# Another order for the side work of a fused cross-attention and expert kernel

## Chip, cores and metric

The kernel runs on one core of a Trainium2 chip. The metric is the device time of one execution in microseconds (us), the median of several runs. The engines are called as the profile calls them: PE (TensorE matmuls; PEld are its weight loads), DVE (VectorE), ACT (ScalarE), POOL (GpSimd) and SP (SyncE, which here only issues transfers).

## What is computed

A tensor x (4 batches, 512 rows, 256 columns) and a context (4 batches, 1601 rows, 256 columns), all in float32, go through two rounds of cross-attention and a mixture of experts:

```python
x = x + L0_xattn(ctx, layernorm(x))   # 8 heads of 128, queries from x, keys and values from ctx and x
x = x + L0_ffn(layernorm(x))          # 8 experts, top 2, capacity, tanh-GELU, 256 -> 1024 -> 256
x = x + L1_xattn(ctx, layernorm(x))   # 8 heads of 32, keys and values from ctx alone
x = x + L1_ffn(layernorm(x))          # 8 experts, top 2 with ties, GELU with biases
```

The second attention, which the change is mostly about, is `softmax(q k^T) v` for 512 queries and 1601 keys in 8 heads, for each of the 4 batches. The second mixture of experts routes each row to its two best experts and adds their weighted results.

## The kernel before, in words

The kernel has four parts that run one after the other, with some work pulled ahead: the first attention (to about 1585 us), the first feed-forward (to 1911 us), the second attention (to about 2537 us), and the second feed-forward (to the end).

**First feed-forward.** `all_experts` runs the 8 experts twice, once for each half of the slots. Per expert it calls `hidden` (32 matmuls and four GELUs on ACT), `turned` for the next expert, and `results` for the one before. After each of these three it takes one step of a generator with side work, so that a half has 24 steps, and one more is taken behind the last `results`. In the second half the generator is `keys_next`: keys and values of batch 1 (15 steps, a yield after every third), the queries of batch 0 (`queries`, 10 yields), and the first ten `maxima` calls. Each call fills two PSUM tiles of the pool `ps_s` with scores and has DVE reduce them to row maxima, which the softmax of the second attention subtracts.

**Second attention.** There are 16 units: batch b, key half o, query half f. Each has 13 steps, one for each block of 128 keys, so that a batch takes 52 steps (`per_batch`) and all four take 208. The loop goes two steps at a time; such a pair is called an iteration here. An iteration issues, in this order: `weights` for its two steps (scores into `ps_w`, then the exponential on ACT), `weigh` for the two steps before (their product with the values, into `ps_o`), `maxima` for a later unit (mostly one call, sometimes two), `add_weights` (two DVE adds that build the softmax sum; steps 0 and 12 of a unit have none), and last whatever is put down in the table `at` for the two steps. The four computing engines keep exactly this written order (`in_order`): an instruction that waits holds all that stands behind it on its engine. Transfers on SP are ordered by the planner.

The side work that `at` holds:

- `closing` of a unit: PE sums, a copy on ACT, PE transposes, three DVE operations into x.
- `keys_values(b + 1)` (generator `projected`): the context of a batch is loaded into `cw`, then 15 steps of matmuls, each into one PSUM tile that ACT copies out.
- `collect(b + 1)` gathers the results of the first experts by indirect DMA on POOL; `add_collected` adds them to x on DVE, one row tile at a time.
- `queries(b + 1)`: a layer norm with its square root on ACT (`ln_root`), PE transposes, two projections. Batch b + 1's are made during batch b.
- `route2(b - 1)`: the routing of the finished batch: layer norm, transposes, logits, top two, places, and 16 indirect scatters on POOL into `rows_a` and `rows_b`.
- `clear_rows`: on steps 4 to 44, transfers that clear these rows, each second one behind a memset on POOL.

The first PSUM tile that side work takes in an iteration comes from a pool of its own (`ps_m`, one buffer); further ones come out of the ring of three of `ps_s`, which `weights` and `maxima` use too (class `Beside`).

**Second feed-forward.** The rows of its first two experts are fetched from `rows_a` at step 202 (`load_first_rows`), turned at step 206 (`turn_first`), and put through the first layer at steps 210 and 213 (`first_layer`). Then 21 tiles of rows follow: for each, `hidden`, preparations of the next, and `results` of the one before, whose two products are scaled on DVE and added to the output by an indirect DMA on POOL (`add_out`). `route2` of the last batch and a planning table run beside. In this part, and in the first feed-forward, a planner chooses the order of instructions on each engine from when it thinks that inputs will be ready; `tc.keep_in_program_order(ins)` holds one instruction behind everything written before it for its engine.

Of the kernel before, what the change touches and what calls it, by code (L numbers as in the profile page):

```python
# [10 lines left out]
AF = mybir.ActivationFunctionType  # L11
# [6 lines left out]
B, S, D = 4, 512, 256  # L18
M = 1601
NT = S // P  # L20
# [20 lines left out]
FC = FF // P  # L41
# [33 lines left out]
def xattn_ffn_twice(ctx: ExitStack, tc: tile.TileContext, a: dict, out: bass.AP):  # L75
    nc = tc.nc
# [60 lines left out]
        nc.vector.tensor_scalar(ve, mv[:, :, 1], EPS, None, ALU.add)  # L137
        return ve

    def ln_root(pool, mv, n, ve=None):  # L140
        if ve is None:
            ve = ln_variance(pool, mv, n)
        rs = pool.tile([P, n], F32, tag=f"rs{n}", name="rs")
        nc.scalar.activation(rs, ve, AF.Sqrt)
        return ve, rs

    def ln_scale(pool, mv, n, root=None):
# [258 lines left out]
    def route2(b, two, psum, tag, first=0, n=NT):  # L406
# [7 lines left out]
        ve = ln_variance(two, mv, n)  # L414
        yield

        root = ln_root(two, mv, n, ve)
        yield
        mv, rs = ln_scale(two, mv, n, root)
        yield  # L420
# [707 lines left out]
    def queries(b, qT):  # L1128
        xn = soon.tile([P, NT, D], F32, tag="xn", name="xn")
        mv = ln_moments(turns, x[b], NT, some=())  # L1130
        for i in range(NT):
            ln_moments(turns, x[b], NT, mv=mv, some=(i,))
            if i + 1 < NT:
                yield
        ve = ln_variance(turns, mv, NT)
        yield

        root = ln_root(turns, mv, NT, ve)
        yield
        mv, rs = ln_scale(turns, mv, NT, root)  # L1140
        for i in range(NT):
            ln_apply(xn, x[b], mv, rs, i)
            if i in (0, NT - 1):
                yield
        xnT = soon.tile([P, DC, S], F32, tag="xnT", name="xnT")
        transposed(banks["beside"], "s", xnT, xn, NT)
        yield
        for o in range(DC):
            ps = banks["beside"].tile([P, 512], F32, tag="s", name="ps_q1")
            for c in range(DC):  # L1150
                nc.tensor.matmul(
                    ps,
                    lhsT=wT[:, 0, c, o * P : (o + 1) * P],
                    rhs=xnT[:, c, :],
                    start=c == 0,
                    stop=c == DC - 1,
                )
            nc.scalar.activation(qT[:, o, :], ps, AF.Copy, scale=DH1**-0.5)
            yield

    kvs = []
# [3 lines left out]
    def load_queries(u):  # L1165
        b, o, f = units[u]
        for pair in range(2):
            for s in range(2):
                i = 2 * pair + s
                nc.sync.dma_start(  # L1170
                    asked[u % 3][64 * s : 64 * s + 32, pair, :],
                    qTs[b][i * DH1 : (i + 1) * DH1, o, f * QH : (f + 1) * QH],
                )
# [60 lines left out]
    def begin(b):  # L1234
        qTs[b] = turns.tile([P, DC, S], F32, tag="qT", name="qT")
# [6 lines left out]
    with ExitStack() as st:  # L1242
# [30 lines left out]
        def hidden(e, half, sxT, w1, w2):  # L1273
            hT = two.tile([P, FC, HALF], F32, tag="hT", name="hT")
            for f0 in range(0, FC, 2):
                ps = ps_h.tile([P, 2, HALF], F32, tag="h", name="ps_h")
                for f in range(2):
                    for c in range(DC):
                        nc.tensor.matmul(  # L1279
                            ps[:, f, :],  # L1280
                            lhsT=w1[:, c, (f0 + f) * P : (f0 + f + 1) * P],
                            rhs=sxT[:, c, :],
                            start=c == 0,
                            stop=c == DC - 1,
                        )
                nc.scalar.activation(hT[:, f0 : f0 + 2, :], ps, AF.Gelu_apprx_tanh)  # L1286
            return e, half, hT, w2
# [86 lines left out]
        def keys_next():  # L1374
            *kv, steps = keys_values(ps_s, "s", 1)
            kvs.append(kv)
            for k, f in enumerate(steps):
                if k == 6:
                    add_collected(0, got0)
                f()  # L1380
                if k % 3 == 2:
                    yield
            begin(0)
            for _ in queries(0, qTs[0]):
                yield
            load_queries(0)
            for g in range(len(pieces)):
                maxima(0, g)
                yield
            negated(0)  # L1390
            for g in range(3):
                maxima(1, g)
                yield
                if g == 0:
                    to_row(0)
# [11 lines left out]
    def hidden_some(w, xT, hT, f0, ps):  # L1407

        n = xT.shape[-1]
        for f in range(2):  # L1410
            for c in range(DC):
                at = c * FF + (f0 + f) * P
                nc.tensor.matmul(
                    ps[:, f, :n],
                    lhsT=w(at, P),
                    rhs=xT[:, c, :],
                    start=c == 0,
                    stop=c == DC - 1,
                )
        for f in range(2):  # L1420
            nc.scalar.activation(
                hT[:, f0 + f, :], ps[:, f, :n], AF.Gelu, bias=w(WB2 + f0 + f, 1)
            )
# [6 lines left out]
    with ExitStack() as st:  # L1430
# [161 lines left out]
        def put(step, *fs):  # L1592
            at.setdefault(step, []).extend(fs)

        def spread(step, gen, every=1, count=8):
            for k in range(count):
                put(step + k * every, lambda: next(gen, None))
# [3 lines left out]
        def place(step, gen, offsets):  # L1601
            for k in offsets:
                put(step + k, lambda: next(gen, None))
            ends.append(gen)

        for u in range(1, n_units):

            put(NM * u - 7, lambda u=u: negated(u))
            put(NM * u - 5, lambda u=u: to_row(u))
            put(NM * u - 12, lambda u=u: load_queries(u))  # L1610
        for b in range(B):
            s0 = per_batch * b
            if b:
                put(s0 - 10, lambda b=b: load_keys(b, 0))
                put(s0, lambda b=b: load_keys(b, 1))

                beside = (4, 8, 10, 18, 20, 22, 24, 28, 30, 32, 34, 36, 38, 40, 42, 44, 46)
                bare = (4, 8, 10, 12, 12, 14, 14, 16, 18, 20, 22, 24, 26, 28, 30, 32, 34)
                steps = beside if b + 1 < B else bare
                place(s0, route2(b - 1, one, side, "s"), (*steps, *range(steps[-1] + 2, 54, 2), *range(54, 62)))  # L1620
            if b + 1 < B:
                put(s0 + 1, lambda b=b: begin(b + 1))
                got, steps = collect(b + 1)

                for k, f in enumerate(steps):
                    put(max(s0 - 28, 0) + 1 + k, f)
                for t in range(NT):
                    put(
                        s0 + 10 + 2 * t,
                        lambda b=b, got=got, t=t: add_collected(b + 1, got, (t,)),  # L1630
                    )

                def later(b=b):
                    yield from queries(b + 1, qTs[b + 1])

                place(s0, later(), range(12, 32, 2))
            if 1 <= b and b + 1 < B:

                def projected(b=b):
                    *kv, steps = keys_values(side, "s", b + 1, nc.scalar.copy)  # L1640
                    kvs.append(kv)
                    yield
                    for f in steps:
                        f()
                        yield

                spread(s0 + 2, projected(), 2, 16)
        put(per_batch * (B - 1) + 4, load_first_weights)
        put(NM * n_units - 6, load_first_rows)
        put(NM * n_units - 2, turn_first)  # L1650
# [58 lines left out]
    with ExitStack() as st:  # L1709
# [61 lines left out]
            turned_rows(rows, xT, tp)  # L1771
            return xT

        def hidden(w, xT, two=two):

            n = xT.shape[-1]
            hT = two.tile([P, FC, G], F32, tag="hT2", name="hT2")[:, :, :n]
            for f0 in range(0, FC, 2):
                hidden_some(w, xT, hT, f0, ps_h.tile([P, 2, G], F32, tag="h", name="ps_h2"))
            return hT  # L1780

# [190 lines left out]
        next(rest)  # L1972
        for i in range(n):
            w, xT, to, share = here
            hT = hidden(w, xT) if i else first_h
            for _ in range(3):
                next(rest, None)
            if more:
                fetched.append(more.pop(0)())
            if i + 1 < n:  # L1980
                here = ready(*fetched.pop(0))
            next(rest, None)
            if last:
                results(*last)
            next(rest, None)
            last = (w, to, share, hT, T - S if i < E else T)
            if i == n - 3:

                counts_i = one.tile([P, 4], I32, name="counts_i")
                tc.keep_in_program_order(nc.vector.tensor_copy(counts_i, state["counts"]))  # L1990
# [129 lines left out]
```

## Time and profile before

| what | value |
|---|---|
| median of 3 runs | 2819.07 us (2818.01 to 2824.54) |
| the profiled execution | 2825.64 us, of which the span of the trace is 2823.9 us |
| mean granted PE clock | 0.983 |
| PE busy | 2711.7 us, 96% of the span |
| DVE busy | 1458.4 us, 52% |
| ACT busy | 939.3 us, 33% |
| POOL busy | 262.4 us, 9% |
| exponentials of the second attention (208), on ACT | first at 1914.4 us, last at 2521.4 us |
| ACT table loads before the root in `ln_root` (line 144) | 20, of 1283 ns each |

PE's share is an average over parts with different limits, so it does not say where time can be won; the second attention has to be read by batch and by iteration. A trace row gives the start, the duration, engine, line, operation and tiles, and in brackets how long the engine had been idle before and what ended that. The page's own chain of waits covers only the last transfers of this program (each of its shares is 0%), so that stretches and single waits of the trace are read instead.

### The profile page before, as it was taken

To read this page: it belongs to the slowest core of one execution; us is meant where nothing else is said; L and a number is where in the kernel's file an instruction comes from. 1 tells how busy PE (TensorE), PEld (TensorE's weight loads), DVE (VectorE), ACT (ScalarE), POOL (GpSimd) and SP (SyncE) were. 2 spreads that over 40 slices of the span, in tenths; PEclk is the share of its full clock that TensorE was granted. 3 is DMA by queue.
4 is the path that set the end of the run, shared out by engine and by line. 5 is a ranking of instruction groups with operands and counts; after the bars stand their busy time and mean duration, and the time that the engine had idled before them with its cause. 6 is when DMAs were issued, how large, how long until landed. Compare 5 with 4: busy or idle time off the path is not lost. (4 is left out here: it accounts for less than half of the span.)

```text
span 2823.9 us, 35983 instructions
## 1 busy us (share of the span) xinstructions
PE 2711.7 (96%) x13566; PEld 1853.8 (66%) x13566; DVE 1458.4 (52%) x2307; ACT 939.3 (33%) x1362; POOL 262.4 (9%) x292
## 2 busy tenths in 40 slices
PE   6999999999999999999999999998999998889998
PEld 3667676666666676666676687874454454458887
DVE  6444556544476445455444412137887878872111
ACT  4323234232333233332332211114444444442221
POOL 0000000100001000001000001001110202022542
PEclk9999999999999999999999999999999999999999
DMA  5444343433343433334434555525621111025573
GB/s 172 116 112 116 97 113 86 111 95 92 93 120 89 106 96 95 96 82 107 98 91 125 166 174 172 173 80 156 176 68 40 38 30 56 31 77 188 163 219 103
DMA packets 196435, 311.95 MB, mean 110 GB/s; under 512 B 43319, under 2 KB 117368, under 8 KB 193560
## 3 DMA queue, kind: packets, MB, share of 16 engines
q1 hardware_dynamic: 157512, 227.52, 29.4%
q0 software_dynamic: 14160, 46.31, 5.6%
q10 hardware_dynamic: 24576, 35.68, 4.9%
q8 instruction: 111, 1.82, 0.3%
q14 instruction: 76, 0.62, 0.1%
HBM read 111.73 MB, written 51.34 MB: 58 GB/s over the span
## 5 line engine op out<-in xcount | busy, mean ns | idle before, releaser
L852 DVE TENSOR_REDUCE top<-ps_s 128x1 f32<-128x2113 f32 x128 | 301.8, 2358 | 587.3 <-PE ps_s L844 587.3
L881 PE MATMUL ps_o<-pT,v 128*128 128x256 f32 x2176 | 521.6, 381 | 0.5 <-DVE inv L859 0.5
L844 PE MATMUL ps_s<-kT,qT 128*128 128x512 f32 (+1 forms) x1280 | 489.0, 526 | 5.8 <-ACT attn L858 5.8
L881 PEld LDWEIGHTS ps_o<-pT,v 128*128 128x128 f32 x2176 | 409.9, 191 | 115.2 <-issue 68.4
L858 ACT ACTIVATE attn<-ps_s,top 128x2113 f32<-128x2113 f32 x128 | 259.0, 2024 | 478.8 <-DVE top L852 435.3
L844 PEld LDWEIGHTS ps_s<-kT,qT 128*128 128x128 f32 x1280 | 241.6, 190 | 252.4 <-issue 237.2
L873 DVE STREAM_TRANSPOSE pT<-swapped 128x2176 f32<-128x2176 f32 x128 | 312.4, 2440 | 33.4 <-DMA swapped<-attn 22.7
L1205 DVE TENSOR_REDUCE tops<-ps_s 128x2 f32<-128x1024 f32 (+1 forms) x224 | 238.3, 1105 | 107.4 <-PE ps_s L1194 106.3
L793 PE MATMUL ps_k<-kvin,wkv 128*128 128x512 f32 (+1 forms) x640 | 262.7, 533 | 3.8 <-DVE mv_g L731 2.1
L1463 PE MATMUL ps_w<-asked,keyed 64*128 64x256 f32 (+1 forms) x1664 | 227.8, 408 | 35.0 <-DVE tops L1205 35.0
L827 PE MATMUL ps_v<-wkv,kvin 128*128 128x256 f32 x1088 | 254.6, 381 | 1.3 <-ACT v L834 1.3
L1476 ACT ACTIVATE pT<-ps_w 128x1024 f32<-128x1024 f32 x192 | 189.8, 1022 | 154.1 <-PE ps_w L1463 138.5
L827 PEld LDWEIGHTS ps_v<-wkv,kvin 128*128 128x128 f32 x1088 | 204.7, 190 | 36.8 <-ACT v L834 6.3
L1463 PEld LDWEIGHTS ps_w<-asked,keyed 64*128 64x128 f32 (+1 forms) x1664 | 151.6, 189 | 113.4 <-DVE tops L1205 55.6
L1481 DVE TENSOR_TENSOR sum<-sum,pT 128x1024 f32<-128x1024 f32 x176 | 214.7, 1220 | 13.5 <-PE ps_o L1490 4.9
L806 ACT ACTIVATE kT<-ps_k,bqk 128x512 f32<-128x512 f32 (+1 forms) x160 | 96.8, 620 | 262.9 <-PE ps_k L793 122.4
L793 PEld LDWEIGHTS ps_k<-kvin,wkv 128*128 128x128 f32 x640 | 115.8, 191 | 77.6 <-issue 67.0
L834 ACT COPY v<-ps_v 128x512 f32<-128x512 f32 x144 | 79.7, 560 | 216.6 <-PE ps_v L827 148.3
L1194 PE MATMUL ps_s<-kv,qT 32*128 32x512 f32 (+1 forms) x1024 | 137.0, 561 | 8.8 <-DVE tops L1205 5.1
L1279 PE MATMUL ps_h<-sxT,w 128*128 128x256 f32 x512 | 116.1, 384 | 4.0 <-ACT hT L1286 4.0
L1293 PE MATMUL ps_y<-w,hT 128*128 128x256 f32 x512 | 116.8, 384 | 0.0
L1279 PEld LDWEIGHTS ps_h<-sxT,w 128*128 128x128 f32 x512 | 97.9, 192 | 20.8 <-ACT hT L1286 4.8
(306 smaller groups left out, 2516.1 us busy)
## 6 DMA issues: line engine op xcount, KB each, us to landing
swapped<-attn SPq DMA_DIRECT2D x1536, 68.0 KB
swapped<-attn ACTq DMA_DIRECT2D x512, 68.0 KB
w<-in_w_dram SPq DMA_DIRECT2D x32, 1024.0 KB
rows_b<-empty SPq DMA_DIRECT2D x36, 530.0 KB
w_e<-in_wall_dram SPq DMA_DIRECT2D x5, 2052.0 KB
cw<-in_ctxT_dram SPq DMA_DIRECT2D x4, 1601.0 KB
keyed<-kv SPq DMA_DIRECT2D x32, 200.1 KB
ctx_b<-in_ctx_dram SPq DMA_DIRECT2D x3, 1536.0 KB
```

What stands on the lines that cost most here:

```text
L793: nc.tensor.matmul(ps[:, :n], lhsT=wkv[:, c, hs], rhs=kvin[:, c, : NB - 1, k, :] if k < 4 else kvin[:, c, NB - 1, :, :], start=c == 0, sto ...
L827: nc.tensor.matmul(ps[:, k, :], lhsT=flat_kvin[c][:, j * P : (j + 1) * P], rhs=wkv[:, c, cols], start=c == 0, stop=c == DC - 1,)
L844: nc.tensor.matmul(flat[:, j0 : j0 + n], lhsT=qT[:, t * P : (t + 1) * P], rhs=kT[:, j0 : j0 + n], start=True, stop=True,)
L852: nc.vector.tensor_reduce(top, flat[:, :L], AX.X, ALU.max, negate=True)
L858: nc.scalar.activation(attn[:, :L], flat[:, :L], AF.Exp, bias=top, accum_out=total)
L873: nc.vector.transpose(pT[:, :, k * P : (k + 1) * P].rearrange("p c (a i) -> p a c i", a=4), swapped.rearrange("p a (c i) -> p a c i", i=32),)
L881: nc.tensor.matmul(ps, lhsT=v[:, j - parts[part][0], (h % 2) * DH0 : (h % 2 + 1) * DH0], rhs=pT[:, j, :], start=j == 0, stop=j == NB - 1,)
L1205: nc.vector.tensor_reduce(tops[u][:, t : t + at // n, 2 * pair : 2 * pair + 2, j0 // 512], of, AX.X, ALU.max,)
L1279: nc.tensor.matmul(ps[:, f, :], lhsT=w1[:, c, (f0 + f) * P : (f0 + f + 1) * P], rhs=sxT[:, c, :], start=c == 0, stop=c == DC - 1,)
L1463: nc.tensor.matmul(ps[:r, s, pair * QH : (pair + 1) * QH], lhsT=keyed[o][64 * s : 64 * s + 64, pair, j * P : j * P + r], rhs=asked[u % 3][ ...
L1476: nc.scalar.activation(pT[:r], ps[:r], AF.Exp)
L1481: nc.vector.tensor_tensor(sums[u, 0], sums[u, 0], pT, ALU.add)
```

## The change

Five things change.

1. **Second attention, keys and values.** The 15 steps of `keys_values` move from every second step (4 to 32 of a batch) to every third (6 to 48). Their generator is now `project`.
2. **Second attention, queries.** In batch 0, queries of batch 1 stay where they were (steps 10 to 34). Those of batch b + 1 for b of 1 and 2 begin 12 steps before batch b instead of 12 steps into it, with the adds of collected rows ahead of them; the gathers move by one step. `begin`, which takes the query tile, moves along (generator `ask`).
3. **Second attention, routing.** `route2` begins at step 0 of a batch instead of 4 and goes on in even steps; for the last batch it ends 6 steps earlier in the written order, at 45 instead of 52.
4. **First feed-forward.** `keys_next` yields after every fourth key step instead of every third, and the square root in the layer norm of batch 0's queries is kept behind what is written before it on ACT (`behind`).
5. **Second feed-forward.** The square root in the last batch's routing is kept in the same way. For the last tile of rows, `results` of the one before is called in the middle of `hidden`, after four of eight column groups, instead of behind it.

```diff
-    def ln_root(pool, mv, n, ve=None):
+    def ln_root(pool, mv, n, ve=None, behind=False):
...
-        nc.scalar.activation(rs, ve, AF.Sqrt)
+        root = nc.scalar.activation(rs, ve, AF.Sqrt)
+        if behind:
+            tc.keep_in_program_order(root)
...
-        root = ln_root(two, mv, n, ve)
+        root = ln_root(two, mv, n, ve, behind=b == B - 1)
...
-        root = ln_root(turns, mv, NT, ve)
+        root = ln_root(turns, mv, NT, ve, behind=b == 0)
...
-                if k % 3 == 2:
+                if k % 4 == 3:
                     yield
...
+        def ask(b):
+            begin(b)
+            yield
+            yield from queries(b, qTs[b])
+        def project(b):
+            *kv, steps = keys_values(side, "s", b, nc.scalar.copy)
+            kvs.append(kv)
+            yield
+            for f in steps:
+                f()
+                yield
...
-                beside = (4, 8, 10, 18, 20, 22, 24, 28, 30, 32, 34, 36, 38, 40, 42, 44, 46)
-                bare = (4, 8, 10, 12, 12, 14, 14, 16, 18, 20, 22, 24, 26, 28, 30, 32, 34)
-                steps = beside if b + 1 < B else bare
-                place(s0, route2(b - 1, one, side, "s"), (*steps, *range(steps[-1] + 2, 54, 2), *range(54, 62)))
+                even = (0, 6, 8, 12, 14, 18, 20, 24, 26, 28, 30, 32, 34, 36, 38, 40, 42, *range(44, 62))
+                bare = (0, *range(6, 37, 2), *range(37, 54))
+                place(s0, route2(b - 1, one, side, "s"), even if b + 1 < B else bare)
             if b + 1 < B:
-                put(s0 + 1, lambda b=b: begin(b + 1))
                 got, steps = collect(b + 1)
+                first = s0 + 10 if b == 0 else s0 - 12
                 for k, f in enumerate(steps):
-                    put(max(s0 - 28, 0) + 1 + k, f)
+                    put(first - (9 if b == 0 else 14) + k, f)
                 for t in range(NT):
                     put(
-                        s0 + 10 + 2 * t,
+                        first + 2 * t,
                         lambda b=b, got=got, t=t: add_collected(b + 1, got, (t,)),
                     )
-                def later(b=b):
-                    yield from queries(b + 1, qTs[b + 1])
-                place(s0, later(), range(12, 32, 2))
+                place(first, ask(b + 1), (0, *range(2, 26, 2)))
             if 1 <= b and b + 1 < B:
-                spread(s0 + 2, projected(), 2, 16)
+                place(s0, project(b + 1), (2, *range(6, 51, 3)))
...
-        def hidden(w, xT, two=two):
+        def hidden(w, xT, two=two, between=lambda: None):
...
             for f0 in range(0, FC, 2):
+                if f0 == FC // 2:
+                    between()
...
-            hT = hidden(w, xT) if i else first_h
+            if i == 0:
+                hT = first_h
+            elif i < n - 1:
+                hT = hidden(w, xT)
+            else:
+                hT = hidden(w, xT, between=lambda: results(*last))
+                last = None
```

More of the change, by code (lines that the diff above doesn't have):

```diff
@@ L1615, in xattn_ffn_twice @@
                 put(s0, lambda b=b: load_keys(b, 1))
-                beside = (4, 8, 10, 18, 20, 22, 24, 28, 30, 32, 34, 36, 38, 40, 42, 44, 46)
-                bare = (4, 8, 10, 12, 12, 14, 14, 16, 18, 20, 22, 24, 26, 28, 30, 32, 34)
-                steps = beside if b + 1 < B else bare
-                place(s0, route2(b - 1, one, side, "s"), (*steps, *range(steps[-1] + 2, 54, 2), *range(54, 62)))
+                even = (0, 6, 8, 12, 14, 18, 20, 24, 26, 28, 30, 32, 34, 36, 38, 40, 42, *range(44, 62))
+                bare = (0, *range(6, 37, 2), *range(37, 54))
+                place(s0, route2(b - 1, one, side, "s"), even if b + 1 < B else bare)
             if b + 1 < B:
-                put(s0 + 1, lambda b=b: begin(b + 1))
                 got, steps = collect(b + 1)
+                first = s0 + 10 if b == 0 else s0 - 12
                 for k, f in enumerate(steps):
-                    put(max(s0 - 28, 0) + 1 + k, f)
+                    put(first - (9 if b == 0 else 14) + k, f)
                 for t in range(NT):
                     put(
-                        s0 + 10 + 2 * t,
+                        first + 2 * t,
                         lambda b=b, got=got, t=t: add_collected(b + 1, got, (t,)),
                     )
-                def later(b=b):
-                    yield from queries(b + 1, qTs[b + 1])
-                place(s0, later(), range(12, 32, 2))
+                place(first, ask(b + 1), (0, *range(2, 26, 2)))
             if 1 <= b and b + 1 < B:
[L1639 to L1645, printed above, removed]
-                spread(s0 + 2, projected(), 2, 16)
+                place(s0, project(b + 1), (2, *range(6, 51, 3)))
         put(per_batch * (B - 1) + 4, load_first_weights)
```

## The prediction

> **What bounds it now.** I read the page's busy times first (PE 96% of the span), then the second attention (1911 to 2522 us) batch by batch in the view of busy times by stretch, cut where the first exponential of a batch starts. Columns: length, then busy us of PE, weight loads, DVE, ACT, POOL, the granted clock, DMA.
>
> ```profile
> 1914.40:2053.70 139.30, 126.34 (x1152) 63.96 (x1150) 117.50 (x137) 66.61 (x81) 21.62 (x46) 0.96 0.68 175
> 2053.70:2219.90 166.20, 153.38 (x1322) 85.43 (x1324) 139.25 (x225) 76.87 (x103) 21.12 (x27) 1.00 0.18 48
> 2219.90:2389.10 169.20, 158.05 (x1324) 86.57 (x1324) 136.78 (x223) 76.90 (x103) 17.95 (x16) 0.96 0.11 29
> ```
>
> The middle batches (rows two and three) are 27 and 30 us longer than batch 0, and neither PE nor DVE fills them: they take turns in being late. The same view for one plain iteration (two steps) and a loaded one of batch 1:
>
> ```profile
> 2049.00:2053.70 4.70, 4.22 (x40) 1.90 (x40) 4.59 (x5) 2.04 (x2) 0.10 (x1) 1.00 0.66 186
> ...
> 2142.10:2152.20 10.10, 9.81 (x76) 4.96 (x76) 4.09 (x4) 4.13 (x7) 0.00 (x0) 1.00 0.04 12
> ```
>
> Plain: DVE full, PE stalls. Loaded: PE full, DVE idle for 6 us. An iteration costs its busier engine.
>
> **The spread, worked out.** Prices are distances between starts in the timeline. PE: two ps_w 1.84, two weighings 1.0, one maxima 1.07, so 3.9 plain; a key or value step 1.75; query transposes 1.9, each projection 1.75; routing's transposes 1.9 and logits 1.8; closing 1.03, then 0.65. DVE: two reduces 2.28 and two adds 2.46, so 4.74 plain; a collected tile 1.03; a row tile's moments 0.64; closing 1.15. For each of the 104 iterations I added up what its two steps hold, took the larger sum, and summed. Against the measured lengths (last iteration left out):
>
> | batch | measured | rule before | rule after |
> |---|---|---|---|
> | 0 | 139.3 | 135.1 | 140.8 |
> | 1 | 166.2 | 163.2 | 160.3 |
> | 2 | 169.2 | 163.2 | 155.1 |
> | 3 | 131.4 | 121.7 | 121.4 |
> | sum | 606.1 | 583.2 | 577.6 |
>
> Batch 1, by steps from its start: steps 26 to 31, where query transposes and projections, routing's transposes and logits, key steps and a closing meet, fall from 27.8 to 19.3 (-8.5), and 10 to 19, which lose the next queries' tiles, by 5.3. Steps 6 to 9 rise by 3.2 (projections beside routing and the first keys), 40 to 45 by 5.1 (the queries two ahead, beside the last routing). The rest gives +2.6 net. Batch 2 takes on no queries at its end: hence -8.1; batch 0 takes them on: +5.7. **Taken: -5.6.** The rule leaves 23 us of waits in before; I let them stay. Ends: a better-spread order removes up to a third of each middle batch's excess over 145 us (DVE's own sum there), -14 for two; or new waits take +10.
>
> Moved DMAs. The context load (cw, 1601 KB) waits for the last key step: that moves from step 32 to 48, and the next first use is at 58, five iterations (about 28 us) on; on SP the loads of keys and queries behind it are for steps 65 and later: 0. The gathers of slot_y move one step, the adds that use them from 62 to 40; on POOL they stand between memsets that wait 7 us each, and before's last gather was issued at 2016.7, with the step-40 iteration at 2025: one memset more (2021.8) still precedes step 46 (2040): 0. Without that cover each late gather would hold DVE, some 5 us.
>
> **Routing's scatters (new wait).** Before, the first rows are fetched after six of batch 2's eight rows_a scatters; bare now ends at 45, so step 202 stands behind all eight.
>
> ```profile
> SPq L1580 <- DMA rows_a<-pay,place_a: 6.3, 1, 6.3
> ...
> 2522.23 0.66 PE L1404 MATMUL tp_f<-ident,cw 128*128 128x128 f32 x4
> ```
>
> The first line is SP's wait before the fetch. By POOL's timeline the sixth scatter went at 2507.46, the fetch at 2510.2, and its last reader was done before 2516.3. The first place comes one iteration later (4.3 us: first scatter 2497 instead of 2492.7); at 3.0 per pair the eighth goes at about 2518, lands near 2521, and the fetch is in at 2523.5 to 2526.6, where PE turns the rows at 2522.2. Behind that transpose on PE stand the last weighing and the first expert. **Taken +2** (0 to +4.4).
>
> **The pinned root of batch 0's queries.** ACT, then PE, in the timeline of the first feed-forward:
>
> ```profile
> 1755.02 1.28 ACT L144 ACT_TABLE_LOAD   x1
> 1760.62 0.20 ACT L144 ACTIVATE rs<-ve 128x4 f32<-128x4 f32 x1 [4.32 <-DVE ve L137]
> ...
> 1762.79 3.78 PE L1279 MATMUL ps_h<-sxT,w 128*128 128x256 f32 x8 [3.72 <-ACT hT L1286]
> ```
>
> The root was queued ahead of GELUs whose matmuls were done, and waited there for moments behind gathers. Pinned behind expert 2's work (some 40 us on) it finds its input ready, and ACT is idle 8.5 us between experts' GELUs. **Taken -3.7**, the whole gap; 0 if PE meets the next wait at once, -5 at most.
>
> **Keys in fours.** Two yields fewer put the last maxima inside the last expert instead of behind it:
>
> ```profile
> 1911.11 3.64 PE L1463 MATMUL ps_w<-asked,keyed 64*128 64x256 f32 x16 [2.54 <-DVE tops L1205]
> ```
>
> The 2.54 goes. Next late is the last result's copy (0.69), beside the first weights. But two full maxima now stand side by side, for which PE lost 0.73 idle and 1.1 in stretched matmuls (2.26 against 1.14) at 1850, where before's last such pair is a small and a full one. **Taken -1.2** (-2.5 to 0).
>
> **The last root.** ACT, then PE, where the last feed-forward begins:
>
> ```profile
> 2533.74 1.28 ACT L144 ACT_TABLE_LOAD   x1 [1.21 <-DVE earlier L500]
> 2535.04 0.20 ACT L144 ACTIVATE rs<-ve 128x4 f32<-128x4 f32 x1
> 2535.26 1.28 ACT L1421 ACT_TABLE_LOAD   x1
> 2536.55 0.84 ACT L1421 ACTIVATE cw<-ps_f,w_kv 128x256 f32<-128x256 f32 x2
> ...
> 2537.45 1.11 PE L1404 MATMUL tp<-ident,cw 128*128 128x128 f32 x4 [4.06 <-ACT cw L1421]
> ```
>
> By the rows the detour is 1.28 + 0.20 + 1.28 = 2.8 us: each function starts 1.3 after its load's start. [...] The rows decide: PE gets at most 3.2 (the GELU could start at 2533.4). But expert 1's matmuls (2539.41) also wait for DVE's copy of xT, which stood behind the norm that the root feeds; with that order kept only 0.3 is won. The planner sees a later root and may turn them round. **Taken -2** (-3.2 to -0.3).
>
> **The last results early.** POOL in the timeline of the end:
>
> ```profile
> 2804.50 1.56 POOL L1798 DMA_INDIRECT out_dram<-y,to  x1 [4.24 <-DVE y L1812]
> 2809.04 1.56 POOL L1798 DMA_INDIRECT out_dram<-y,to  x1 [2.98 <-DMA out_dram<-y,to]
> 2813.45 1.56 POOL L1798 DMA_INDIRECT out_dram<-y,to  x1 [2.85 <-DMA out_dram<-y,to]
> ```
>
> Each adding DMA follows the one before by 4.4 to 4.5. Half of hidden (1.86) moves behind results, so the third-last y is ready at 2802 and its DMA goes at 2803.2; then 2807.7 and 2812.2. **-1.2** (0 to -1.5).
>
> **Sum.** -5.6 + 2 - 3.7 - 1.2 - 2 - 1.2 = -11.7. The profiled execution took 2825.64 (span 2823.9 and 1.74 around it), 6.6 above the median of the runs, 2819.07. The same difference gives 2813.9 for it and **2807** for the median.
>
> **Rivals.** (1) *The spread gives nothing*: two sums of some 580 differ by 5.6 where 23 stay unexplained. For it: DVE's total is the same. Then -6, 2813: no change. (2) *It gives more*: PE may run one ps_w ahead of DVE (0.9 us), so lone key steps vanish in DVE's time, and the waits of crowded iterations go with the crowd. A third to a half of the middle batches' excess (21 and 24 us): 2795. Against: projections still meet keys and routing. (3) *Slower: DVE's side work ahead of its reduces.* A later iteration's reduces queue behind it, and PE needs the ps_s buffers that they free:
>
> ```profile
> 2409.46 1.94 PE L1194 MATMUL ps_s<-kv,qT 32*128 32x512 f32 x4 [2.39 <-DVE tops L1205]
> ```
>
> There 2.4 us of moments and closing stood in front. After, some 19 iterations hold queries' tiles beside routing or closing, or two or more side tiles. Five paying 2.4 each cancel the gain, nine make it slower by over 0.3%; ten give 2831. Against: before's steps 10 to 16 of batch 0 hold the same tiles and kept within 3 us of the rule together. (4) *The pins are moot*, the planner leaving both gaps: 2813, within (1).
>
> **Numbers.** A change under 0.3% (8.5 us) is within what runs of this kernel tell apart. Forecast (2801 to 2810.6) 0.36, (2) 0.24, (1) with (4) 0.25, (3) 0.15: faster 0.60, same 0.25, slower 0.15. The range, 2794 to 2824, leaves out a tenth at each side.
>
> **What would show it.** Batches 0 to 2 at about 145, 163 and 161 us; no 10-us iterations at a middle batch's steps 28 to 31; no PE gap at 1759, 1909 or of 4 us near 2533; a gap ahead of tp_f; the last POOL DMAs 4.5 apart. Wrong: batch 1 above 170, or DVE waiting on g.

## The result, and the profile after

The changed kernel takes **2811.86 us**, median of 11 runs (2800.23 to 2820.83), against 2819.64 us for the kernel before in the same comparison (2816.81 to 2826.92): ratio 0.9963, interval 0.995 to 0.9976. It is faster by 0.37%. The two profiled executions stand at 2825.64 and 2816.91 us (spans 2823.9 and 2815.2), both at a mean granted clock of 0.983. Against the -11.7 forecast, the medians differ by -7.8 us and the two spans by -8.7.

Busy times by stretch of the changed kernel, cut as before at the first exponential of each batch (columns as before: length; busy us of PE, weight loads, DVE, ACT, POOL; granted clock; DMA):

```profile
1913.40:2058.30 144.90, 127.26 (x1149) 64.98 (x1151) 123.54 (x155) 69.65 (x84) 22.38 (x51) 0.95 0.65 171
2058.30:2228.70 170.40, 160.22 (x1324) 87.30 (x1322) 137.72 (x224) 76.93 (x105) 27.82 (x33) 0.95 0.19 53
2228.70:2391.90 163.20, 156.47 (x1320) 85.48 (x1316) 130.95 (x206) 74.00 (x101) 16.83 (x16) 0.97 0.10 26
2391.90:2516.40 124.50, 113.14 (x1101) 64.77 (x1103) 109.41 (x179) 61.11 (x76) 17.24 (x15) 0.96 0.13 43
```

Batch 1 (second row) is the surprise: 170.4 us, four more than before, where 163 was forecast. "Batch 1 above 170" was one of the two signs named beforehand of being wrong; the other, DVE waiting on g, did not occur. The column to read beside it is the clock: 0.95, where before's batch 1 had 1.00. Two iterations of it, steps 90 and 96, in the same view:

```profile
2175.40:2187.10 11.70, 9.20 (x54) 4.38 (x56) 10.15 (x18) 3.21 (x4) 0.00 (x0) 0.85 0.04 12
2198.50:2211.50 13.00, 11.82 (x68) 6.58 (x68) 10.44 (x29) 2.53 (x3) 8.76 (x9) 0.68 0.37 110
```

And the timeline of step 90 on PE (start, duration, operation, idle time ahead and its end):

```profile
2178.10 1.14 PE L1197 MATMUL ps_s<-kv,qT 32*128 32x512 f32 x8
2179.72 0.41 PE L510 MATMUL ps_c<-cnt,before 128*128 128x32 f32 x2 [0.49 <-DVE cnt L501]
2181.03 0.41 PE L513 MATMUL ps_c<-earlier,ones 128*128 128x32 f32 x2 [0.89 <-DVE earlier L503]
2181.27 0.60 PE L521 MATMUL tp_w<-ident,wb 128*8 128x128 f32 x4
2182.36 3.50 PE L1062 MATMUL ps_k<-cw 128*128 128x512 f32 x4 [0.49 <-DVE tops L1208]
```

For three microseconds PE does little, because routing's small matmuls wait for a chain on DVE. Then the key step, which takes 1.99 us two iterations later, takes 3.50: the clock record has 0.5 from 2182.7 to 2186.1. In the clock records of the two profiles the granted clock is 1.0 or 0.5 and nothing else (19 halved stretches before, 20 after), and every halved stretch is 3.413, 6.827 or 10.240 us long (but for the one that each record's end cuts off), all of one execution on one grid of 3.413 us, which lies differently against the start of the span: 3.24 us behind it before, 1.56 after.

So I take from each length what the clock took: length times one minus the granted clock, called the **clock's loss** below. For the two profiled executions:

| stretch | before: length, loss, rest | after: length, loss, rest | change of the rest | forecast |
|---|---|---|---|---|
| start to first exponential | 1914.4, 18.6, 1895.8 | 1913.4, 18.8, 1894.6 | -1.2 | -4.9 |
| batch 0 | 139.3, 5.3, 134.0 | 145.0, 6.8, 138.1 | +4.1 | +5.7 |
| batch 1 | 166.2, 0.7, 165.5 | 170.3, 8.5, 161.8 | -3.7 | -2.9 |
| batch 2 | 169.2, 6.1, 163.1 | 163.2, 5.1, 158.1 | -5.0 | -8.1 |
| batch 3, to step 206 | 131.4, 8.5, 122.8 | 124.5, 5.1, 119.4 | -3.4 | -0.3 |
| step 206 to the end | 303.4, 7.5, 296.0 | 298.8, 3.9, 294.8 | -1.2 | -1.2 |
| span | 2823.9, 46.7, 2777.2 | 2815.2, 48.3, 2766.9 | -10.3 | -11.7 |

In this table the rule by which the forecast sized the iterations fits the kernel before to within 2.3 us in every batch (135.1, 163.2, 163.2, 121.7). The "23 us of waits" that it left over are about the clock's loss, 20.6 us.

Of the other signs named beforehand: the 10-us iterations at steps 28 to 31 of the middle batches are gone (steps 80 and 82: 10.02 and 9.93 became 5.06 and 6.44), so is the PE gap at 1759, and there is a gap ahead of tp_f. That gap on PE, and the end of POOL's timeline:

```profile
2519.78 0.90 PE L1407 MATMUL tp_f<-ident,cw 128*128 128x128 f32 x4 [1.55 <-DMA cw<-rows_a]
...
2795.63 1.56 POOL L1805 DMA_INDIRECT out_dram<-y,to  x1 [2.96 <-DVE y L1819]
2800.15 1.56 POOL L1805 DMA_INDIRECT out_dram<-y,to  x1 [2.96 <-DMA out_dram<-y,to]
2804.66 1.56 POOL L1805 DMA_INDIRECT out_dram<-y,to  x1 [2.96 <-DMA out_dram<-y,to]
```

The last three adding DMAs are 4.5 apart and no longer wait for anything but one another: the first of them names DVE, but that y was done at 2794.8, and its distance from the DMA before it (2791.12) is 4.5 too.

### The profile page after: what moved, and what is told of

Read it like the earlier page. It is cut to its first block, busy times and chain, and to the rows that moved or that the text cites. A ratio compares the mean times of both kernels' runs of the same rounds, so it can differ in the third digit from the quotient of the medians.

```text
span 2815.2 us, 35980 instructions
## 1 busy us (share of the span) xinstructions
PE 2714.6 (96%) x13566; PEld 1853.9 (66%) x13566; DVE 1457.6 (52%) x2307; ACT 939.6 (33%) x1362; POOL 258.8 (9%) x292
## 5 line engine op out<-in xcount | busy, mean ns | idle before, releaser
L1296 PEld LDWEIGHTS ps_y<-w,hT 128*128 128x128 f32 x512 | 98.4, 195 | 18.3 <-issue 2.6
```

The lines of the kernel that those rows point to most:

```text
L1296: nc.tensor.matmul(ps[:, t, :], lhsT=hT[:, f, t * P : (t + 1) * P], rhs=w2[:, f, :], start=f == 0, stop=f == FC - 1,)
```

## Experiments

The twelve kernels below ran on three chips, four on each, and on each chip the kernel before was timed beside them: the first chip has both kernels again and the two halves of the change, the second keys ahead of routing, the early fetch, keys in threes and earlier queries, and the third the rest. Lengths of stretches are compared less the clock's loss ("the rest"), where not said otherwise.

### The same kernels again: is it the clock or the load?

No edit. Theory G says that the halved stretches come and go between executions and the rest stays; rival L that the crowd of an iteration sets its length.

The kernel before:

> The kernel before, unchanged, once more. Theory G (the gated TensorE clock): in the records the granted clock is either 1.0 or 0.5, in stretches of 3.41 us or a multiple, and which stretches are halved differs from execution to execution. Take the clock's loss (length times one minus the granted clock) from each length: the rest is the same in every execution. Then the rest is 2775 to 2779 us over the whole span, and 134, 165.5, 163 and 123 us for batches 0 to 3 of the second attention (each within 2), although the raw lengths move by up to 6 us, with halved stretches at other places than in the first profile. Rival L (load alone: the halved clock is where TensorE has nothing to do anyway): the raw lengths come back within 1 us (139.3, 166.2, 169.2, 131.4) and the rest moves.

The changed kernel:

> The changed kernel, unchanged, once more. Theory G: less the clock's loss 2766 to 2771 us over the span, and 138, 162, 158 and 119.5 us for the four batches, each within 2; the raw length of batch 1, 170.3 in the first profile with 8.5 us lost in it, comes out anywhere from 163 to 171, and run times follow the mean clock with some 2.8 us for each 0.001. Rival L: batch 1 comes back at 170 within 1 us because its steps 90 and 96 (11.7 and 13.0 us) are crowded, and the times don't follow the clock.

And once more, on the third chip:

> The changed kernel, unchanged, beside the mended one on the same chip. Theory G: less the clock's loss, the stretch from the second half of the first feed-forward to the first exponential is 158.5 us again, batches 1 and 2 are 160 to 162 and 158, batch 3 119.5 to 120; step 90 takes 11.2 to 11.7 and step 96 either 9.4 (no halved stretch in it) or 12.5 to 13.3 (with one), the difference being the clock's loss. Rival L: step 96 at 12.7 to 13 whatever the clock.

Measured, the kernel before: batches 1 to 3 rest 164.5, 164.4, 122.5, within 1.3 us of the first profile, while the raw lengths moved by +2.4, -0.9 and -1.1: as G has it, by a small margin. Batch 0 missed: 141.0, not 134, and with it the whole span: 2786.6 less the clock's loss, where 2775 to 2779 was expected (the stretch up to the first exponential was 2.7 longer as well). Nearly all of batch 0's excess is in its last iteration (step 50: 14.37 instead of 4.70 us), which the timeline of PE explains:

```profile
2053.94 3.53 PE L1463 MATMUL ps_w<-asked,keyed 64*128 64x256 f32 x16 [8.62 <-DMA asked<-qT]
```

Batch 1's first queries were late: in SP's queue they stand behind the clears of rows_b, which follow each other at 7.4 us on this chip and at 6.9 to 7.3 at the same place in the first profile.

The changed kernel: rests of 160.3, 158.0, 120.2 and 161.4, 158.0, 120.2 for batches 1 to 3 (first profile 161.8, 158.1, 119.4). The range given for raw batch 1 was too narrow, 172.2 and 169.9 with 11.9 and 8.5 us lost. Step 96 took 12.65 and 12.67 in both: by itself that does not tell G from L. What does is the same instruction order in batch 1 in another execution (the experiment with the first rows early, below). The view of stretches for its step 96, to be held against the row of 13.00 us above:

```profile
2195.70:2205.00 9.30, 8.11 (x66) 4.56 (x62) 8.78 (x25) 2.48 (x3) 5.37 (x6) 1.00 0.26 75
```

Clock 1.00 instead of 0.68, and 9.39 instead of 12.97 us from exponential to exponential. The second attention alone had 9.38 there, again with nothing lost. L falls.

Run times follow the clock too: over the 11 runs after, span times clock scatters by 1.7 us (standard deviation), the span itself by 6.4; the slope of span against loss is 0.99. In the runs of the kernel before on the first and third chip that slope is 0.67 and 0.69 (51 and 17 runs), so not all of the loss is paid everywhere, and taking it out in full is an approximation. Their rest is 2781.9 us in both; the changed kernel's is 2771.9 and 2770.1.

### One half of the change at a time

```diff
 # second attention only: this part of the change (main lines), nothing else
...
+        place(s0, route2(b - 1, one, side, "s"), even if b + 1 < B else bare)
...
+        place(first, ask(b + 1), (0, *range(2, 26, 2)))
+        place(s0, project(b + 1), (2, *range(6, 51, 3)))
 # all but the second attention: these (main lines), nothing else
...
+        root = ln_root(two, mv, n, ve, behind=b == B - 1)
...
+        root = ln_root(turns, mv, NT, ve, behind=b == 0)
...
+                if k % 4 == 3:
...
+                hT = hidden(w, xT, between=lambda: results(*last))
```

> The kernel before with the change's placement in the second attention alone (no pinned roots, keys in threes, no early results). My forecast's theory (the placement is worth -5.6 and the rows that wait for all scatters +2): ratio 0.9987, and by the trace of the changed kernel, which shows the second attention 8 us shorter at the full clock, ratio 0.9972 to 0.998. Rival S (the spread gives nothing, the gain comes from the pins and the early results): ratio 1.000 to 1.001, and less the clock's loss 2777 us as before. Batches 0 to 3 less the clock's loss 138, 162, 158, 119.5 in the first case, 134, 165.5, 163, 123 in the second.

> The change without its placement in the second attention: both pinned roots, keys in fours, the last results early. My forecast's terms: -3.7 -1.2 -2 -1.2 = -8.1 us, ratio 0.9971. By the trace of the changed kernel these parts give less (first attention and feed-forward -1.2, the end -1.2 together with the scatters' +2): -2 to -4, ratio 0.9986 to 0.9993. Rival S: -8 to -11, nearly all of the change. Locally: no TensorE gap of 3.7 us near 1759 and none of 4 us at the last feed-forward's start, as in the changed kernel; no gap ahead of tp_f, since the scatters are as before.

Measured: ratio **0.9969** (0.996 to 0.9978) for the second attention alone and **0.9981** (0.9974 to 0.9988) for everything else; both together 0.9953 (0.9936 to 0.997) on the same chip, their product to within 0.03%. The rival by which the spread gives nothing falls. For everything else, both sizes written beforehand missed: it gave less than the forecast's terms (0.9971) and more than the trace of the changed kernel had suggested (0.9986 to 0.9993). Alone, the placement leaves batches 1 to 3 at 162.7, 157.8 and 119.3, and makes the part behind step 206 longer, 300.1 instead of 295.7. Everything else, alone, shortens that part to 293.4 and leaves the stretch from the second half's first transposes to the first exponential as it was in the first profile (158.4; before 158.3 to 159.6 in five profiles).

### Queries alone, routing alone

```diff
 # queries only, in the kernel before (its adds, gathers and query tile move too)
...
-                place(s0, later(), range(12, 32, 2))
+                place(first, ask(b + 1), (0, *range(2, 26, 2)))
 # routing only, in the kernel before (with both new lists of steps)
...
-                place(s0, route2(b - 1, one, side, "s"), (*steps, *range(steps[-1] + 2, 54, 2), *range(54, 62)))
+                place(s0, route2(b - 1, one, side, "s"), even if b + 1 < B else bare)
```

> The kernel before with the queries moved alone (two batches ahead, around the batch's end). By the rule of the busier engine: batches 0 to 3 +5.7, +1.6, -4.5, 0, sum +2.6; less the clock's loss 140, 166.5, 159, 122.5 us. Rival: moving the queries is what brings the gain of batch 2 (-6 to -8) and the sum is below 0.

> The kernel before with routing in even steps alone (both lists). By the rule: batches 0 to 3 0, -2.5, -2.5, -0.3; less the clock's loss 134 to 135, 162, 161, 122. By the trace of the changed kernel, where batch 3 holds nothing but routing and lost 3.4: batch 3 at 119.5. And the gap ahead of tp_f comes with this part: 1.5 to 6 us.

| rest of batches 1, 2, 3 | | sum |
|---|---|---|
| before (two profiles) | 165.5 163.1 122.8; 164.5 164.4 122.5 | 451.4; 451.4 |
| queries alone | 158.8, 161.0, 122.6 | 442.4 |
| routing alone | 159.9, 160.5, 120.4 | 440.8 |
| whole change (three profiles; none on the second chip) | 161.8 158.1 119.4; 160.3 158.0 120.2; 161.4 158.0 120.2 | 439.3; 438.5; 439.6 |

These two kernels ran once each (2830.77 and 2824.90 us, at granted clocks of 0.980 and 0.983), so that only their stretches are compared. By the rule, queries alone should give -2.9 there and routing alone -5.3. They give -9.0 and -10.6: both sizes were wrong, and the rival is right that moving the queries alone gains. (The kernel with all but the second attention, which has before's placement, has 449.9, so single profiles of one placement can differ by 1.5.) Either one already breaks up the pile at steps 80 and 82 (10.02 and 9.93 before; 8.30 and 8.22 with the queries, 8.69 and 8.14 with routing), and together they give -12.3, far less than their sum. Batch 3 comes from routing, as its -2.3 alone shows. So does the new wait (PE, where the first rows are turned, routing alone):

```profile
2520.38 1.18 PE L1404 MATMUL tp_f<-ident,cw 128*128 128x128 f32 x4 [4.75 <-DMA cw<-rows_a]
```

On the second chip this gain is not seen. The three kernels there that keep the changed order of queries, keys and routing (early fetch, keys in threes, earlier queries) have sums of 449.0, 449.6 and 451.6 for batches 1 to 3. No profile of the kernel before was taken on that chip, but the ratios of its two kernels with many runs, 0.9977 and 0.9982, are nearer to 1 as well than the 0.9951 to 0.9963 of the changed kernel elsewhere. Part of the excess is stalls of DVE that no other chip showed (last section); the rest is not explained.

### Keys ahead of routing

```diff
+            if 1 <= b and b + 1 < B:
+                place(s0, project(b + 1), [k - k % 2 for k in (2, *range(6, 51, 3))])
             if b:
                 even = ...
...
-            if 1 <= b and b + 1 < B:
-                place(s0, project(b + 1), (2, *range(6, 51, 3)))
```

> The changed kernel with each key or value step put ahead of the routing step of the same iteration (same iterations, other order on TensorE). Theory W: what the rule of the busier engine missed in batches 1 and 2 is TensorE's waiting behind VectorE's chains (before ps_c and ps_b) and the halved clock that follows such a stretch. Then steps 90 and 142 fall from 11.65 to 9.0 (within 0.7), step 96 from 12.7 to 9, step 148 from 9.7 to 8.5; batches 1 and 2 together lose 7 to 12 us, most of it in the clock's loss, and the ratio to the kernel before goes from 0.9953 to 0.992 to 0.9935. Rival V: VectorE's load sets these iterations (10.1 us busy in step 90), so steps 90 and 142 stay above 10.5 and the time is that of the changed kernel within 2 us.

Steps 90 and 142 fell from 11.7 to 9.24 us both, at full clock, as theory W had it. Of these 2.4 us, 1.7 are the clock's loss and 0.7 the rest. Step 96 came to 9.34, but step 98 caught 3.1 us of halved clock, and step 148 rose to 16.20 instead of falling to 8.5. The ratio, 0.9977 (0.9967 to 0.9988), missed what I had written, and it cannot be set against the changed kernel, which did not run on this chip. The nearest there, the changed kernel with the early fetch (next section), has 0.9982: a gain of the order by itself does not show in the run times. Step 148 is that chip's: it took 16.8 us with keys in threes and with earlier queries as well, which keep the changed kernel's order there.

### The first rows' fetch

```diff
-        put(NM * n_units - 6, load_first_rows)
+        put(NM * n_units - 10, load_first_rows)
```

> The changed kernel with the fetch of the first expert's rows four steps earlier, behind six scatters as in the kernel before. My forecast sized that wait at +2 (0 to +4.4). Theory: it is the TensorE gap ahead of tp_f (1.55, 5.98 and 3.31 us in the three profiles with the new placement), and a long one is followed by the halved clock; without it no gap ahead of tp_f, the stretch from the last iteration (step 206) to the end falls from 298.8 and 306.2 to 294 to 298, and less the clock's loss to 293.5 (within 1), as without the placement. Rival: TensorE meets the next wait at once (the first expert's weights): the stretch stays at 295 or above less the clock's loss.

No gap ahead of tp_f, and from step 206 to the end a rest of 293.3 us, as expected (the length, 298.5, is just above the 294 to 298 written). But this run proves little: on this chip batch 3 was held up elsewhere, and two kernels with the late fetch had no gap either (rests 293.4 and 293.5). The ratio is 0.9982 (0.9969 to 0.9996). On the third chip the wait is there to be removed, below.

### Keys in threes, and earlier queries

```diff
 # keys in threes
-                if k % 4 == 3:
+                if k % 3 == 2:
 # asked early
-            put(NM * u - 12, lambda u=u: load_queries(u))
+            put(NM * u - (20 if u == 4 else 12), lambda u=u: load_queries(u))
```

> The changed kernel with the first keys in threes again, as before. Forecast: undoing it costs 1.2 us between the second half's start and the first exponential (167.8 to 169.0), with the gap of 2.5 us ahead of ps_w back. By the gaps of the changed kernel's trace (2.54 became 0.88, but 1.32, 0.79 and 1.49 are new) undoing it gains 0.4: 167.4, less the clock's loss in both.

> The changed kernel with batch 1's first queries fetched eight steps earlier (unit 4's load at step 32 instead of 40). Theory: on this chip batch 1's first matmuls wait for these loads, which stand in SyncE's queue between the clears of rows_b (7.3 us each): the kernel before waits 8.6 us there, the changed one 2.8 and runs then at half clock. Then steps 50 and 52 fall from 7.40 and 7.29 to 5 to 6 and 4.0, no TensorE gap over 1 us ahead of ps_w near them; 4 to 5 us in all. Rival: the keys' loads in the same queue come last and the gap stays.

Keys in threes: from the first transposes of the second half (4 to 5 us behind the mark that the expectation uses) to the first exponential the rest is **155.4 us**. All seven profiles with the change's fours have 158.4 to 158.5. Undoing this part gains 3.1 us, not 0.4, and does not cost 1.2 (one execution, 2821.81 us; the mended version below has 156.2, a gain of 2.3). In the changed kernel:

```profile
1890.04 2.26 PE L1197 MATMUL ps_s<-kv,qT 32*128 32x512 f32 x8 [1.31 <-DVE tops L1208]
1901.87 7.17 PE L1296 MATMUL ps_y<-w,hT 128*128 128x256 f32 x32 [0.79 <-DVE y L1304]
1909.92 2.00 PE L1466 MATMUL ps_w<-asked,keyed 64*128 64x256 f32 x16 [0.88 <-DVE y L1304]
1914.47 1.13 PE L1197 MATMUL ps_s<-kv,qT 32*128 32x512 f32 x4 [1.49 <-ACT sum L1479]
```

and with threes:

```profile
1905.87 3.52 PE L1466 MATMUL ps_w<-asked,keyed 64*128 64x256 f32 x16 [2.54 <-DVE tops L1208]
```

The one big gap is bought off with four smaller ones. Gaps above 0.3 us between 1850 and 1916 sum to 5.2 against 3.3 us; the other 1.2 of the 3.1 I have not located.

Asked early: inconclusive (one execution, 2829.29 us). On this chip there was no wait at batch 1's start in any of the four kernels (step 52: 4.01), so there was nothing to win.

### A mended version

The three repairs at once: keys ahead of routing, keys in threes, the first rows' fetch early.

```diff
-                if k % 4 == 3:
+                if k % 3 == 2:
...
-                place(s0, project(b + 1), (2, *range(6, 51, 3)))
+                place(s0, project(b + 1), [k - k % 2 for k in (2, *range(6, 51, 3))])   # ahead of route2
...
-        put(NM * n_units - 6, load_first_rows)
+        put(NM * n_units - 10, load_first_rows)
```

> The changed kernel with the three repairs that the runs point to: key and value steps ahead of routing on TensorE, the first keys in threes, the first rows' fetch behind six scatters. By the profiles: keys in threes -3.1 less the clock's loss (158.5 to 155.4) and up to -1.5 of halved clock at steps 2 to 8; keys ahead of routing -2 to -6 (steps 90, 142, 96); the fetch -1 to -6 where TensorE waits for it. Together -6 to -13 us against the changed kernel, ratio to the kernel before 0.991 to 0.994. Rival: repairs trade one wait for the next and the ratio stays that of the changed kernel (0.995 to 0.9965).

**2796.25 us**, ratio **0.9876** to the kernel before (0.9861 to 0.989), where the changed kernel on the same chip has 0.9951 (0.9935 to 0.9967): better than either, and by more than I had written. The three repairs were not timed apart on this chip. Steps 90 and 96 of its profile, then its PE at the first rows:

```profile
2168.20:2177.50 9.30, 7.31 (x56) 4.08 (x58) 8.85 (x17) 3.25 (x5) 0.00 (x0) 1.00 0.05 14
2189.00:2198.00 9.00, 8.21 (x66) 4.64 (x62) 8.52 (x23) 2.48 (x3) 5.80 (x6) 1.00 0.25 76
```

```profile
2503.56 0.66 PE L1407 MATMUL tp_f<-ident,cw 128*128 128x128 f32 x4
```

and the changed kernel there, same chip:

```profile
2515.92 0.45 PE L1407 MATMUL tp_f<-ident,cw 128*128 128x128 f32 x1 [4.50 <-DMA cw<-rows_a]
```

Between these two profiles batch 1 falls from 169.9 to 163.1 us with its rest unchanged (161.4), so all of that is clock (step 148, though, took 9.46 instead of 8.23, so not every crowded iteration gains); and step 206 to the end from 303.6 to 296.7, of which 3.2 is the wait (rest 295.3 to 292.1) and 3.6 the clock's loss. Over all runs the rest falls by 7.2 us (2770.1 to 2762.9) and the mean clock rises from 0.9838 to 0.9885, which is as much again and more.

## Why the prediction was right, and where it was wrong

The total was right: -11.7 forecast; by medians -7.8 in the result and -12.9 and -14.3 on the first and third chip; less the clock's loss -10.3 in the first pair of profiles, -10.0 and -11.8 in the means of the runs on those chips. Its terms were less so, and that they sum to the right figure is partly luck.

- **The spread, -5.6.** Right in direction and in sum, but not in its sizes. For batches 1 to 3 the rule gave -11.3; -12.3 was measured (451.4 to a mean of 439.1), as -3.8, -5.7 and -2.7 instead of -2.9, -8.1 and -0.3. The size for batch 3 failed because nothing there is priced but sums, while routing's lone waits (step 162: 9.76 to 6.80) went. The parts were mis-sized: queries alone gave -9.0 and not -2.9, routing alone -10.6 and not -5.3. The gain is no sum over queries, keys and routing, since any one mover thins the same pile; so "an iteration costs its busier engine" fits the kernel before and the whole change, but not the steps between, and the near agreement of -11.3 with -12.3 is partly errors of opposite sign.
- **Batch 0, +5.7.** Measured +4.1 in the first pair. On the first chip -1.6: there, the kernel before waits at the batch's end for transfers in SP's queue, and the added work fills that wait. "Moved DMAs: 0" held, but I read SP's queue as covered on the strength of one execution.
- **"The rule leaves 23 us of waits in before; I let them stay."** The step that failed. By the batch they match not waits between engines but the halved clock, 20.6 us of it, to within 2.3 us. Hence the forecast had no term for what the change does to the clock, and batch 1 came out at 170.3. The granted clock stood in the rows that I showed (0.96, 1.00, 0.96).
- **Rival 3**, side work on DVE ahead of its reduces: the mechanism is there, at steps 90 and 96, but where the order of issue was changed alone, steps 90 and 142 fell by 2.4 us each (11.7 to 9.24), of which 1.7 is the clock's loss. Step 96 lost 2.5 to 4.4 us to the clock in five profiles with the old order and none in two others, and at step 148 the new order did not help. That makes four such iterations, not nine.
- **Scatters, +2.** The wait is real; under-sized. Placement alone +4.4 and routing alone +4.3 in the rest, +6 in length, since behind a gap of 3.31 to 5.98 us PE ran as at the halved clock (16 weighing matmuls took 1.93 to 1.94 us there, 1.07 ahead of the gap, and 1.07 behind the gap of 1.55). In the changed kernel the gap was 1.55, 5.98 and 4.50 us. (Routing's end, at step 45 instead of 52, moved by seven steps, not six.)
- **Pinned root of batch 0's queries, -3.7.** Right: with fours taken out again, 155.4 and 156.2 against a mean of 159.1 in five profiles without the pin, -3.3.
- **Keys in fours, -1.2.** Wrong in sign: +2.3 and +3.1. I named the price of two full maxima side by side and set it off only in part against the gap.
- **The last root, -2, and the last results, -1.2.** Right. Without the new scatters' wait, step 206 to expert 1's first matmul falls from 18.9 to 15.4 us, of which 1.75 is clock's loss; from there to the end 284.5 to 283.3, rest -0.7. The planner did turn the copy of xT ahead of the norm:

```profile
2532.10 0.66 PE L1407 MATMUL tp<-ident,cw 128*128 128x128 f32 x4 [0.93 <-ACT cw L1424]
2532.86 0.69 DVE L1408 COPY xT<-tp 128x512 f32<-128x512 f32 x1 [1.41 <-PE tp L1407]
2533.36 0.20 ACT L145 ACTIVATE rs<-ve 128x4 f32<-128x4 f32 x1
```

In short: fours gave back what the pin won, the scatters' wait what the tail won, and what is left, some 10 us, is the second attention's spread; on the second chip less of it was to be seen.

## What to carry to other kernels

Read the granted clock of a stretch before explaining its length, and compare stretches with the clock's loss taken out; on the first and third chip what remains repeats to a tenth of a microsecond in more than 90 of 103 iterations of the second attention, where the run time moves by 20 us. On an engine with a fixed order, put the work whose inputs are ready ahead of the work that waits for another engine's chain: at steps 90 and 142 the same instructions took 2.4 us less each, 1.7 of it because the clock stayed up. When work is moved, follow each transfer behind it to its first reader.

## What the hardware showed that was not expected

- A halved clock does not need an idle PE. In the profiles of the kernel before and of the first changed one, between 1913 and 2530 us, all nine stretches of the 3.413-us grid in which PE was busy for less than half (30 to 47%) were followed by a halved one, even the one ahead of step 90's key step (2179.3 to 2182.7, 46% busy), in which no gap is over 0.9 us. Of the 36 stretches between half and three quarters busy, nine were. Yet in the changed kernel three halved ones followed stretches at clock 1.0 that the records call full (100% busy; from 2138.3, 2309.0 and 2370.4): at steps 78, 130 and 148, where the order holds logits or the thin ps_b matmuls. Busy time alone thus does not tell when the clock is halved; what does, the runs do not settle.
- On the second chip DVE stood still for 6.9 us at step 148 in three of four kernels, and for 9.2 at step 194 in the fourth. With earlier queries its input was written by 2369.6, and DVE began at 2375.2. The waits of DVE (waited for, us in total, times, longest) in that profile, from 2360 to 2390:

```profile
DVE tops L1208 <- remote: 7.2, 2, 6.9
DVE tops L1208 <- PE ps_s L1197: 6.2, 2, 5.4
```

"Remote" is a release that the profile cannot place. ACT has such waits in these profiles too (6.3 and 4.0 us with the early fetch, up to 3.7 with earlier queries), and PE, with earlier queries, one of 2.90 us without a releaser up to 2375.7, while POOL issues the scatters. Between 1913 and 2530 us no profile of another chip has such a wait of DVE, and its cause stays open.
